# Two node tiles moved from a one-hot product to gathers, the last tile moved to the front, and index lists kept in DRAM

## The chip, the core and the metric

The kernel runs on one core of a Trainium2 chip. The metric is the device time of one execution, in microseconds; every comparison is made with runs of the kernel before on the same chip. The core has a matrix engine (PE, with its weight loads shown apart as PEld), a vector engine (DVE), an activation engine (ACT), a general engine (POOL) that issues the indirect DMAs here, and a sync engine (SP) that issues the plain ones. Each of them works through its own list of instructions strictly in order and waits on semaphores of the others.

## What is computed

The input is a graph of 6250 nodes with 256 features and 200,000 edges sorted by destination. The parts of the reference that matter:

```python
xn = layernorm(x)
x  = x + gcn(edge_index, xn) + linear_attention_block(xn)   # gcn: sum over edges, then W, b, relu
x  = x + mixture_of_experts(layernorm(x))                   # 8 experts, each node goes to one, 977 slots each
# gcn: deg = edges into a node + 1; norm = dinv[src] * dinv[dst]
#      out[n] = relu( sum over edges e into n (and a self loop) of (xn @ W)[src[e]] * norm[e] + b )
```

The sum over the edges is the costly part: for each node, about 32 rows of 256 features from anywhere in the graph have to be added.

## The kernel before

The nodes are cut into 49 tiles of 128 (the last, tile 48, has 106). Tiles are handled in pairs: pair 0 is tiles 0 and 1, pair 23 is tiles 46 and 47, and pair 24 is tile 48 alone. The run has three stages.

**First stage (to about 300 us).** `first_passes` makes the attention sums and queries, pair by pair. `first_chain`, interleaved with it, finds where each node's edges begin (`search`), scales the node features and splits them into bf16 parts (`graph_rows`), and makes the edge lists (`edge_lists`): for gathered tiles `idx` (the source row of each edge) and `rel` (its destination within the tile), for dense tiles `hiT` and `loT` (two numbers that name an edge's source tile and row). All four lists are in SBUF. `checked` counts what would break the fast path into one flag; a branch on that flag ends the stage. With this input the slow path behind the flag is not taken.

**Main stage (about 300 to 1645 us).** Three Python generators are stepped in turn by the loop at the end of the block, and that order is the order in which each engine meets the work (`tc.manual_schedule`):

- `gather()` does the 24 odd tiles. A tile has up to `EB = 34` groups of 128 edges, so there are 24 x 34 = 816 steps. In each step POOL issues one indirect DMA that fetches 128 rows of 2 KB from `g_dram` into `gt` (L891), DVE makes a one-hot matrix `oh` (L895), and `LAG = 7` steps later PE adds `oh` x `gt` to the tile's sum `ps` (L906). `gt` and `oh` have `GB = 9` buffers. `ps` takes one bank of PSUM and has two buffers. A tile begins with two matmuls with an identity for the self loop (L903, L904). `put_sum` takes a finished sum out: an ACT copy (L825) and a DVE add (L827).
- `dense()` does the 25 even tiles. It builds the count matrix A of a tile (49 source tiles x 128 x 128): DVE makes one-hots `lo` and `hi` (L838, L840), 44 of each for a tile, PE multiplies them into `bp` (L874, two buffers, 44 matmuls), and ACT casts `bp` into A (L875, 22 casts). For the tile before it, PE runs the 147 matmuls of A with the features `xs3` (L858). The one-hots are made one step ahead of the matmuls that use them, in 8 buffers of each kind. There are 11 steps to a tile.
- `rounds()` does, for each pair, attention output, feed-forward, graph-layer output, routing logits; every second pair `routing()` finds the expert slot of each node, and POOL scatters the rows to `xbuf` (L984). A round for pair c waits until both tiles of c are summed. Pairs go from 0 to 24.

For each `gather` step the loop runs as many `dense` steps as keep the two in proportion, and `SIDE = 0.74` steps of `rounds`. [...] `mps` 3, `gaps` (for `ps`) 2, `deps` (for `ps_d`) 1, `bups` (for `bp`) 2.

**Last stage (from about 1690 us).** All scatters to `xbuf` have to have landed (`main.close()`); then the eight experts are run, each on its 977 slots, and their rows are scattered to the output. The change does not touch it.

Of the kernel before, what the change touches and what calls it, by code (L numbers as in the profile page):

```python
# [37 lines left out]
ND = (NB + 1) // 2  # L38
NDC = ND // 5
GN = 6  # L40
NG = 22
HID = NB * GN // 2
NGB = NB // 2
# [3 lines left out]
GB = 9  # L47
LAG = 7
SIDE = 0.74
# [13 lines left out]
def graph_block_kernel(  # L63
# [32 lines left out]
    deg_dram = dram.tile([AGR, 1], F32, name="deg_dram")  # L96
    q_dram = dram.tile([len(twos), P, 2, 2 * P], F32, name="q_dram")
# [3 lines left out]
    lists = main.enter_context(tc.tile_pool(name="lists", bufs=1))  # L101
    idx = lists.tile([P, NGC * P], I32, name="idx")
    rel = lists.tile([P, NGC * P], F32, name="rel")
    hiT = lists.tile([P, NDC, 2, 5 * NG], F32, name="hiT")
    loT = lists.tile([P, NDC, 2, 5 * NG], F32, name="loT")
# [136 lines left out]
    V.tensor_scalar(goff, goff, float(EB), float(P), op0=OP.add, op1=OP.mult)  # L242
    nfirst = raw.tile([P, NGC], F32, name="nfirst")
    V.tensor_scalar(nfirst, nth, 2.0 * P, -float(P), op0=OP.mult, op1=OP.add)
# [217 lines left out]
    def edge_lists():  # L462


        fb_ps = sm_ps[:, 64:64 + NGB]
        nc.tensor.matmul(fb_ps, sel0, begin[:, 1:2 * NGB:2], start=True, stop=True)
        fb = raw.tile([P, NGB], F32, name="fb")
        V.tensor_copy(fb, fb_ps)
# [11 lines left out]
        for k, (v, w) in enumerate(((begin, NDC), (pid, NDC), (size, 1))):  # L480
            o = sm_ps[:W, 128 + 16 * k:128 + 16 * k + w]
            for b in range(5):
                rhs = v if w == 1 else v[:, 2 * b:NB:10]
                nc.tensor.matmul(o, sel5[:, b].rearrange("p a g -> p (a g)"), rhs, start=(b == 0), stop=(b == 4))
            t = raw.tile([P, w], F32, name=f"picked{k}")
            V.tensor_copy(t[:W], o)
            picked.append(t)
# [30 lines left out]
        for c in range(NGC):  # L518
            if c % 4 == 0:
                et = [rps.tile([P, 512], F32, name="et_ps", tag="et_ps", bufs=2) for _ in range(2)]  # L520
            gd, gs = got.pop(c)
            gf, gf2 = gd.bitcast(F32), gs.bitcast(F32)
            V.tensor_scalar(gf, gd, nfirst[:, c:c + 1], None, op0=OP.subtract)
            V.tensor_copy(gf2, gs)
            yield
            for e, w in zip(et, (gf, gf2)):
                nc.tensor.transpose(e[:, c % 4 * P:(c % 4 + 1) * P], w, ident)
            ask(c + 2)
            yield
            if c % 4 == 3 or c == NGC - 1:  # L530
                for o, e in zip((rel, idx), et):
                    nc.scalar.copy(o[:, (c - c % 4) * P:(c + 1) * P], e[:, :(c % 4 + 1) * P])
                yield
        for c in range(NDC):
# [18 lines left out]
            for v, o in ((kf, hiT), (lf, loT)):  # L553
# [3 lines left out]
                nc.scalar.copy(o[:, c].rearrange("p h g -> p (h g)"), et_ps[:, :2 * W])  # L557
# [4 lines left out]
    def checked():  # L562
# [12 lines left out]
        wide = raw.tile([1, NGB], F32, name="wide")  # L575
        V.tensor_tensor(wide, begin[:1, 2:2 * NGB + 1:2], begin[:1, 1:2 * NGB:2], op=OP.subtract)
# [131 lines left out]
    with tc.If(flag == 1):  # L708
        with tc.tile_pool(name="gp", bufs=1, side="right") as gp:
# [96 lines left out]
            V.memset(rel, -1.0)  # L806
            V.memset(hiT, 400.0)
# [3 lines left out]
    with tc.tile_pool(name="ga", bufs=GB, side="right") as ga, \  # L811
            tc.tile_pool(name="de", bufs=2, side="right") as de, \
            tc.tile_pool(name="gaps", bufs=2, space=PSUM) as gps, \
            tc.tile_pool(name="deps", bufs=1, space=PSUM) as dps, \
            tc.tile_pool(name="bups", bufs=2, space=PSUM) as bps, \
# [5 lines left out]
        def put_sum(t, ps):  # L821
# [4 lines left out]
            if t % 2:  # L826
                V.tensor_tensor(sums[gi][:, 1, :], ps[:, D:], sums[gi][:, 1, :], op=OP.add)  # L827
            there.add(t)

        def onehots(u, p):  # L830

            c, b = divmod(u, 5)
            o = []
            for g in (2 * p, 2 * p + 1):
                for h in range(2):
                    col = b * NG + g
                    lo = de.tile([P, P], BF16, name="lo", tag="lo", bufs=8)
                    V.tensor_scalar(lo, rowb, loT[:, c, h, col:col + 1], None, op0=OP.is_equal)  # L838
                    hi = de.tile([P, NB * GN], BF16, name="hi", tag="hi", bufs=8)
                    V.tensor_scalar(hi, hib, hiT[:, c, h, col:col + 1], None, op0=OP.is_equal)  # L840
                    o.append((lo, hi))
            return o

        def dense():

            mats, made = {}, None
            acc_ps = None
            half = NG // 2
            for u in range(ND + 1):
                for p in range(half):  # L850
                    if u >= 1 and p >= 1:

                        A = mats[u - 1]
                        if p == 1:
                            acc_ps = dps.tile([P, D], F32, name="ps_d", tag="ps_d")
                        for hi in range((p - 1) * NB // (half - 1), p * NB // (half - 1)):
                            for h in range(3):
                                nc.tensor.matmul(acc_ps, A[:, hi, :], xs3[:, hi, h * D:(h + 1) * D],  # L858
                                                 start=(hi == 0 and h == 0), stop=(hi == NB - 1 and h == 2))
                    coming = None  # L860
                    if u < ND:
                        if p == 0:
                            mats[u] = de.tile([P, NB, P], BF16, name="A", tag="A")
                        coming = (u, p, onehots(u, p))
                    if made is not None:
                        uu, pp, oh = made
                        for i in range(2):
                            g = 2 * pp + i
                            w = GN if g < NG - 2 else 4
                            at = GN * g if g < NG - 1 else P - 4  # L870
                            bp = bps.tile([P, 512], F32, name="bp", tag="bp")
                            for h in range(2):
                                lo, hi = oh[2 * i + h]
                                nc.tensor.matmul(bp[:, :NB * GN], lo, hi, start=(h == 0), stop=(h == 1))  # L874
                            nc.scalar.copy(mats[uu][:, :, at:at + w],  # L875
                                           bp[:, :NB * GN].rearrange("p (s k) -> p s k", k=GN)[:, :, :w])
                        if pp == half - 1:

                            V.tensor_tensor(mats[uu][:, 2 * uu, :], mats[uu][:, 2 * uu, :], identb, op=OP.add)
                    made = coming  # L880
                    if u >= 1 and p == half - 1:
                        put_sum(2 * (u - 1), acc_ps)
                    yield

        def gather():
            tiles = {}
            ps = None
            for j in range(NGT + LAG):
                if j < NGT:
                    gt = ga.tile([P, 2 * D], FR, name="gt", tag="gt")  # L890
                    nc.gpsimd.indirect_dma_start(  # L891
                        out=gt, out_offset=None, in_=g_dram,
                        in_offset=bass.IndirectOffsetOnAxis(ap=idx[:, j:j + 1], axis=0))
                    oh = ga.tile([P, P], FR, name="oh", tag="oh")
                    V.tensor_scalar(oh, rowb, rel[:, j:j + 1], None, op0=OP.is_equal)  # L895
                    tiles[j] = (gt, oh)
                i = j - LAG
                if i >= 0:
                    k, e = divmod(i, EB)
                    t = 2 * k + 1  # L900
                    if e == 0:
                        ps = gps.tile([P, 2 * D], F32, name="ps", tag="ps")
# [11 lines left out]
        def routing(batch, lgt, slots):  # L914

            tiles = [(gi, i) for gi in batch for i in range(twos[gi][1])]
            m = len(tiles)
            t0 = twos[batch[0]][0]
# [5 lines left out]
            def a3(name):  # L924
                return small([P, 4, N_EXP], name)[:, :m, :]

            def a2(name):
                return small([P, 4], name)[:, :m]
# [24 lines left out]
            fore = small([P, 5, N_EXP], "fore")  # L953
# [20 lines left out]
            for gi in batch:  # L974
# [5 lines left out]
            put = small([P, 4], "put", dtype=I32)  # L980
# [10 lines left out]
        def rounds():  # L991


            NGR = len(twos)
            xts, qs, ss, slots = {}, {}, {}, {}
            lgt = None

            def load(gi):
                if gi < NGR:
# [19 lines left out]
            for k in range(-2, NGR):  # L1019
                a = k + 2 if k + 2 < NGR else None  # L1020
                b = k + 1 if 0 <= k + 1 < NGR else None
                c = k if k >= 0 else None
# [3 lines left out]
                if a is not None:  # L1026
                    load(a + 1)
# [48 lines left out]
                if c is not None:  # L1076
                    slot = slots[c] = mx.tile([P, 2, ROW], F32, name="slot", tag="slot", bufs=3)
# [65 lines left out]
                if c is not None:  # L1143
# [5 lines left out]
                    if lgt is None:  # L1149
                        lgt, batch = small([P, 4, N_EXP], "lgt"), []  # L1150
                        if cr < P:
                            V.memset(lgt, 0.0)
                    at = 2 * len(batch)
                    batch.append(c)
# [5 lines left out]
                if c is not None:  # L1160
                    V.tensor_tensor(lgt[:cr, at:at + cn, :], lp[:cr, :cn * N_EXP].rearrange("p (t e) -> p t e", e=N_EXP),
# [12 lines left out]
                if c is not None and (len(batch) == 2 or c == NGR - 1):  # L1174
# [4 lines left out]
        n_dense = (ND + 1) * (NG // 2)  # L1179
# [11 lines left out]
        while any(alive.values()):  # L1191
            step("g", G)
            while alive["d"] and done_d * (NGT + LAG) < n_dense * (j + 1):
# [147 lines left out]
```

## Time and profile before

| | |
|---|---|
| median of 3 runs | 2057.87 us (2054.58 to 2075.5) |
| the profiled execution | 2051.43 us, span of its instructions 2049.6 us |
| main stage, first gather to last gather matmul | 302.1 to 1645.1 us |
| between last gather matmul and first instruction of the last stage | 1645.1 to 1689.3 us |
| busy in 300 to 1645 us: PE, DVE, POOL, ACT | 1097.8, 965.2, 841.0, 407.8 us |
| indirect gathers on POOL | 816, median 0.94 us |

"Busy" is the time in which an engine has an instruction of its own running, taken from one profiled execution. Issue of plain DMAs, waits and branches are not counted. Two instructions of PE that overlap count once, so a busy time is a union; the "mean ns of one" beside it is longer than the union divided by the count, since matmuls are pipelined. A line such as "L874 PE MATMUL bp<-hi,lo" names the line of the code, the engine, the operation, and the tile it writes from the tiles it reads.

### The profile page before, as it was taken

Reading aid. Unit: us, or ns where it says so; the run is one execution under the profiler, and the core shown is the slowest. Engines: PE = TensorE matmul, PEld = TensorE weight load, DVE = VectorE, ACT = ScalarE, POOL = GpSimd, SP = SyncE. Lnnn points to the kernel's source line nnn. Section 1 sums busy time; section 2 is a strip of 40 time slices with the busy share of each in tenths; the row PEclk is TensorE's granted clock in tenths of the full one; section 3 lists DMA queues with packets and bytes.
Section 4 is the critical chain, followed back from the end, with each engine's and each line's share of the span. In section 5 each row is a group of like instructions: output and inputs, shape, how many; then the busy total and the mean of one; then the engine's idle time right before and its main releaser. Section 6 shows DMA issues by size and latency. Waiting matters only on the chain. (4 is left out here: it accounts for less than half of the span.)

```text
span 2049.6 us, 28653 instructions
## 1 busy us (share of the span) xinstructions
PE 1648.4 (80%) x9171; PEld 1203.4 (59%) x9171; DVE 1275.3 (62%) x5337; ACT 700.4 (34%) x1627; POOL 924.3 (45%) x957
## 2 busy tenths in 40 slices
PE   5787866887888888887878787887878737999996
PEld 2454544666666666665656565665656525586774
DVE  5767657677767778686757677776867431232332
ACT  2657952233333333232323232332323112233332
POOL 1022006666666666656656666665665610011111
PEclk9888997999998989898989899898999958999998
DMA  7346767777776677767767676667676615414220
GB/s 214 100 133 196 253 182 194 181 183 196 184 187 173 182 182 189 194 161 193 187 180 180 183 181 169 171 185 183 171 179 170 172 35 188 174 49 146 99 96 19
DMA packets 211319, 337.83 MB, mean 165 GB/s; under 512 B 30047, under 2 KB 79002, under 8 KB 211018
## 3 DMA queue, kind: packets, MB, share of 16 engines
q0 software_dynamic: 125424, 232.93, 44.3%
q1 hardware_dynamic: 85434, 101.74, 15.5%
q8 instruction: 81, 1.33, 0.3%
q10 hardware_dynamic: 288, 1.08, 0.1%
q14 instruction: 92, 0.75, 0.1%
HBM read 278.29 MB, written 60.06 MB: 165 GB/s over the span
## 5 line engine op out<-in xcount | busy, mean ns | idle before, releaser
L891 POOL DMA_INDIRECT gt<-g_dram,idx x816 | 794.8, 974 | 576.1 <-issue 168.7
L858 PE MATMUL ps_d<-xs,A 128*128 128x256 bf16 x3675 | 489.4, 287 | 41.3 <-issue 37.5
L875 ACT CAST A<-bp 128x294 bf16<-128x294 f32 (+1 forms) x550 | 200.6, 401 | 832.8 <-PE bp L874 231.0
L858 PEld LDWEIGHTS <-A 128*128 128x128 bf16 x3675 | 355.5, 103 | 171.5 <-issue 112.9
L906 PE MATMUL ps<-gt,oh 128*128 128x512 f32 x816 | 335.1, 484 | 42.6 <-DMA gt<-g_dram,idx 32.3
L840 DVE TENSOR_SCALAR hi<-hib,hiT 128x294 bf16<-128x294 bf16 x1100 | 351.0, 323 | 1.1 <-issue 1.1
L874 PE MATMUL bp<-hi,lo 128*128 128x294 bf16 x1100 | 216.0, 305 | 120.2 <-ACT A L875 39.6
L838 DVE TENSOR_SCALAR lo<-rowb,loT 128x128 bf16<-128x128 bf16 x1100 | 269.9, 245 | 3.2 <-PE ps_d L858 1.2
L895 DVE TENSOR_SCALAR oh<-rowb,rel 128x128 fp32r<-128x128 bf16 x816 | 207.2, 288 | 76.2 <-remote 30.4
L874 PEld LDWEIGHTS <-lo 128*128 128x128 bf16 x1100 | 109.6, 102 | 180.9 <-issue 57.3
L906 PEld LDWEIGHTS ps<-gt,oh 128*128 128x128 f32 x816 | 153.3, 206 | 76.5 <-DMA gt<-g_dram,idx 37.4
L1285 POOL DMA_INDIRECT out<-rep,who x43 | 42.4, 986 | 314.7 <-DVE rep L1283 226.8
L1257 PE MATMUL hpf<-xet,w1e 128*128 128x512 f32 (+2 forms) x544 | 154.1, 441 | 8.7 <-ACTq L1297 3.5
L1267 PE MATMUL ypf<-w2e,hm 128*128 128x256 f32 (+1 forms) x688 | 151.3, 379 | 0.0
L1267 PEld LDWEIGHTS ypf<-w2e,hm 128*128 128x128 f32 (+1 forms) x688 | 128.9, 188 | 21.9 <-issue 3.1
L1257 PEld LDWEIGHTS hpf<-xet,w1e 128*128 128x128 f32 x544 | 86.5, 193 | 70.0 <-issue 62.9
L1269 DVE TENSOR_TENSOR y<-ypf,fb_s 128x256 f32<-128x256 f32 (+1 forms) x43 | 18.2, 423 | 138.8 <-PE ypf L1267 138.8
L662 PE MATMUL mm<-wqkv_s,xnt 128*128 128x512 f32 (+1 forms) x196 | 101.5, 644 | 0.0
L1259 ACT ACTIVATE hm<-hpf,fb_s 128x512 f32<-128x512 f32 (+2 forms) x136 | 70.9, 525 | 84.6 <-PE hpf L1257 81.2
L1051 DVE TENSOR_SCALAR z<-mm 128x8 f32<-128x8 f32 (+1 forms) x49 | 7.9, 162 | 138.6 <-remote 82.6
L984 POOL DMA_INDIRECT xbuf<-slot,put x49 | 51.8, 1058 | 74.5 <-issue 45.4
L1101 ACT ACTIVATE s<-s,nb,rs 128x256 f32<-128x256 f32 (+1 forms) x98 | 53.6, 599 | 47.3 <-DVE rs_sr L194 29.8
(289 smaller groups left out, 2034.1 us busy)
## 6 DMA issues: line engine op xcount, KB each, us to landing
gt<-g_dram,idx POOLq DMA_INDIRECT x816
g_dram<-two SPq DMA_DIRECT2D x24, 512.0 KB
xt<-in_x SPq DMA_DIRECT2D x42, 256.0 KB
xbuf<-zeros SPq DMA_DIRECT2D x26, 384.0 KB
xe<-xbuf SPq DMA_DIRECT2D x8, 1028.0 KB
w1e<-in_fw SPq DMA_DIRECT2D x8, 1024.0 KB
w2e<-in_fw SPq DMA_DIRECT2D x8, 1024.0 KB
xe<-xbuf SPq DMA_DIRECT2D x8, 771.0 KB
```

Of the source, the lines that this page charges most:

```text
L662: nc.tensor.matmul(kp[:r, :], xnt[:, c, i * r:i * r + r], wqkv_s[:, c, D:3 * D], start=(c == 0), stop=(c == 1))
L838: V.tensor_scalar(lo, rowb, loT[:, c, h, col:col + 1], None, op0=OP.is_equal)
L840: V.tensor_scalar(hi, hib, hiT[:, c, h, col:col + 1], None, op0=OP.is_equal)
L858: nc.tensor.matmul(acc_ps, A[:, hi, :], xs3[:, hi, h * D:(h + 1) * D], start=(hi == 0 and h == 0), stop=(hi == NB - 1 and h == 2))
L874: nc.tensor.matmul(bp[:, :NB * GN], lo, hi, start=(h == 0), stop=(h == 1))
L875: nc.scalar.copy(mats[uu][:, :, at:at + w], bp[:, :NB * GN].rearrange("p (s k) -> p s k", k=GN)[:, :, :w])
L891: nc.gpsimd.indirect_dma_start(out=gt, out_offset=None, in_=g_dram, in_offset=bass.IndirectOffsetOnAxis(ap=idx[:, j:j + 1], axis=0))
L895: V.tensor_scalar(oh, rowb, rel[:, j:j + 1], None, op0=OP.is_equal)
L906: nc.tensor.matmul(ps, oh, gt, start=False, stop=(e == EB - 1))
L1257: nc.tensor.matmul(hp[:, :nn], w1e[:, c, f * P:(f + 1) * P], xet[:, c, at:at + nn], start=(c == 0), stop=(c == 1))
L1259: nc.scalar.activation(hm[:, f, :nn], hp[:, :nn], AF.Relu, bias=fb1_s[:, e * 8 + f:e * 8 + f + 1])
L1267: nc.tensor.matmul(yp[:r, :], hm[:, f, (i - i0) * P:(i - i0) * P + r], w2e[:, f, :], start=(f == 0), stop=(f == DFF // P - 1))
```

## The change

1. Tiles 16 and 32 go from `dense` to `gather`. The tile lists are written out as `GTS` (26 gathered tiles) and `DTS` (23 dense ones), and all index arithmetic that relied on odd and even tiles is replaced (`ahead`, `gone`, `columns_of`, `pid_d`, `begin_d`; the check of widths goes over all tiles).
2. Tile 48 is the first dense tile and its pair the first round. Its logits and its slot row wait in tiles of their own (`lgt_h`, `slot_h`) and join the routing of the last two pairs, so that the last routing has 5 tiles.
3. The lists go from SBUF to DRAM in the first stage (ACT copies into a staging tile `st`, SP writes it out) and come back in pieces during the main stage (`gather_lists`, `dense_lists`: 128 gather steps or 5 dense tiles at a time, two buffers).
4. Buffers and distances: `GB` 9 to 11, `LAG` 7 to 9, one-hots of `dense` made two steps ahead in 12 buffers instead of one step ahead in 8, `bp` three banks instead of two, `ps` one bank instead of two. Between two gathered tiles `gather()` yields once more, so one turn of the loop has no gather. `SIDE` is 0.72.

```diff
+GTS = [t for t in range(NB) if t % 2 or t in (16, 32)]
+DTS = [t for t in range(NB) if t not in GTS]
+ND = len(DTS)
...
+    ahead = raw.tile([P, NGB], F32, name="ahead")
+    V.memset(ahead, 2.0)
+    for k in range(NGB):
+        if GTS[k] - (GTS[k - 1] if k else 0) == 1:
+            V.memset(ahead[:, k:k + 1], 1.0)
...
+    V.tensor_tensor(gone, past, ahead.unsqueeze(1).to_broadcast([P, NGC, NGB]), op=OP.mult)
+    V.tensor_reduce(nfirst, gone, AX.X, OP.add)
+    V.tensor_scalar(nfirst, nfirst, float(P), None, op0=OP.mult)
+    def columns_of(o, v, ids):
+        k = 0
+        while k < len(ids):
+            step = max(1, ids[k + 1] - ids[k]) if k + 1 < len(ids) else 1
+            m = k + 1
+            while m < len(ids) and ids[m] - ids[m - 1] == step:
+                m += 1
+            V.tensor_copy(o[:, k:m], v[:, ids[k]:ids[m - 1] + 1:step])
+            k = m
...
-GB = 9
-LAG = 7
-SIDE = 0.74
+GB = 11
+LAG = 9
+SIDE = 0.72
...
-                for o, e in zip((rel, idx), et):
-                    nc.scalar.copy(o[:, (c - c % 4) * P:(c + 1) * P], e[:, :(c % 4 + 1) * P])
+                for o, e in zip((rel_l, idx_l), et):
+                    st = rw.tile([P, 512], F32, name="st", tag="st")
+                    st = st[:, :(c % 4 + 1) * P] if o is rel_l else st[:, :(c % 4 + 1) * P].bitcast(I32)
+                    nc.scalar.copy(st, e[:, :(c % 4 + 1) * P])
+                    nc.sync.dma_start(o[:, (c - c % 4) * P:(c + 1) * P], st)
...
-                nc.scalar.copy(o[:, c].rearrange("p h g -> p (h g)"), et_ps[:, :2 * W])
+                st = rw.tile([P, 512], F32, name="st", tag="st")
+                nc.scalar.copy(st[:, :2 * W], et_ps[:, :2 * W])
+                nc.sync.dma_start(o[:, c, :], st[:, :2 * W])
...
-            tc.tile_pool(name="gaps", bufs=2, space=PSUM) as gps, \
+            tc.tile_pool(name="gaps", bufs=1, space=PSUM) as gps, \
             tc.tile_pool(name="deps", bufs=1, space=PSUM) as dps, \
-            tc.tile_pool(name="bups", bufs=2, space=PSUM) as bps, \
+            tc.tile_pool(name="bups", bufs=3, space=PSUM) as bps, \
...
+        def part(name, source, dtype=F32):
+            t = chunks.tile([P, source.shape[-1]], dtype, name=name, tag=name)
+            nc.sync.dma_start(t, source)
+            return t
...
+        def dense_lists(c):
+            if c < NDC:
+                his[c] = part("hiT", hi_l[:, c, :]), part("loT", lo_l[:, c, :])
+        def gather_lists(c):
+            if c < NGC:
+                idxs[c] = (part("idx", idx_l[:, c * P:(c + 1) * P], I32), part("rel", rel_l[:, c * P:(c + 1) * P]))
+        gather_lists(0)
+        dense_lists(NDC - 1)
+        dense_lists(0)
+        gather_lists(1)
+        def node_tile(u):
+            return DTS[(u - 1) % ND]
...
+            for n in range((ND + 1) * half + 2):
+                u, p = divmod(n, half)
+                if u < ND:
+                    if p == 0:
+                        mats[u] = de.tile([P, NB, P], BF16, name="A", tag="A")
+                    made.append((u, p, onehots(u, p)))
+                m = n - 2
...
-                    t = 2 * k + 1
+                    t = GTS[k]
                     if e == 0:
+                        if k:
+                            yield
                         ps = gps.tile([P, 2 * D], F32, name="ps", tag="ps")
...
+            order = [NGR - 1] + list(range(NGR - 1))
...
-                a = k + 2 if k + 2 < NGR else None
-                b = k + 1 if 0 <= k + 1 < NGR else None
-                c = k if k >= 0 else None
+                a = order[k + 2] if k + 2 < NGR else None
+                b = order[k + 1] if 0 <= k + 1 < NGR else None
+                c = order[k] if k >= 0 else None
...
+                    if c == NGR - 2:
+                        V.tensor_copy(lgt[:, 4, :], lgt_h)
+                        batch.append(NGR - 1)
...
-                if c is not None and (len(batch) == 2 or c == NGR - 1):
+                if c is not None and cn > 1 and len(batch) >= 2:
                     yield from routing(batch, lgt, slots)
...
-        n_dense = (ND + 1) * (NG // 2)
+        n_dense = (ND + 1) * (NG // 2) + 2
+        n_gather = NGT + LAG + NGB - 1
```

## The prediction

> **What bounds the kernel now.** I read the page's first two parts, then busy time by stage, then who waited for whom on PE and on POOL inside the main stage, then a timeline of POOL, and last the chain that ended last.
>
> Busy time by stage (columns: stretch in us, its length, busy of PE, PEld, DVE, ACT, POOL with counts, granted PE clock, DMA share, GB/s):
>
> ```profile
> 300.00:1645.00 1345.00, 1097.76 (x6926) 827.81 (x6926) 965.23 (x4396) 407.76 (x970) 841.04 (x860) 0.91 0.70 181
> 1645.00:1690.00 45.00, 13.99 (x45) 9.50 (x43) 18.04 (x93) 6.12 (x12) 5.61 (x5) 0.51 0.07 23
> 1690.00:2049.60 359.60, 318.67 (x1360) 230.19 (x1360) 94.87 (x229) 108.02 (x211) 42.40 (x43) 0.95 0.32 110
> ```
>
> The main stage is 1345 of 2050 us, and in it no engine is full: PE is busy 82%. The 45 us after it are nearly empty. The costliest groups of the main stage:
>
> ```profile
> L891 POOL DMA_INDIRECT gt<-g_dram,idx x816 | 794.8, 974 | 576.1 <-issue 168.7
> L858 PE MATMUL ps_d<-xs,A 128*128 128x256 bf16 x3675 | 489.4, 287 | 41.3 <-issue 37.5
> L906 PE MATMUL ps<-gt,oh 128*128 128x512 f32 x816 | 335.1, 484 | 42.6 <-DMA gt<-g_dram,idx 32.3
> L840 DVE TENSOR_SCALAR hi<-hib,hiT 128x294 bf16<-128x294 bf16 x1100 | 351.0, 323 | 1.1 <-issue 1.1
> L874 PE MATMUL bp<-hi,lo 128*128 128x294 bf16 x1100 | 216.0, 305 | 120.2 <-ACT A L875 39.6
> L838 DVE TENSOR_SCALAR lo<-rowb,loT 128x128 bf16<-128x128 bf16 x1100 | 269.9, 245 | 3.2 <-PE ps_d L858 1.2
> L895 DVE TENSOR_SCALAR oh<-rowb,rel 128x128 fp32r<-128x128 bf16 x816 | 207.2, 288 | 76.2 <-remote 30.4
> ```
>
> Who PE and POOL waited for, in 300 to 1645 us:
>
> ```profile
> PE bp L874 <- ACT A L875: 39.6, 26, 3.3
> PE ps_d L858 <- issue: 37.5, 49, 2.2
> PE ps L906 <- DMA gt<-g_dram,idx: 32.3, 24, 2.7
> PE bp L874 <- DVE lo L838: 17.0, 12, 8.5
> PE bp L874 <- DVE hi L840: 14.7, 14, 2.1
> ...
> POOL gt L891 <- PE ps L906: 140.7, 132, 4.4
> ```
>
> PE loses 247 us (1345 - 1098) in short stalls: a bank of `bp` not yet emptied by ACT, one-hots not yet made by DVE, gathered rows not yet landed. POOL mostly waits for PE to free a `gt` buffer. So PE's in-order list with its stalls sets the pace. POOL is the next limit: back to back it issues a gather every 1.24 us,
>
> ```profile
> 1617.07 0.94 POOL L891 DMA_INDIRECT gt<-g_dram,idx  x1 [0.30 <-issue]
> 1618.31 0.94 POOL L891 DMA_INDIRECT gt<-g_dram,idx  x1 [0.31 <-issue]
> ```
>
> and with the mean (0.974 + 0.30 us of issue, and 1.35 for each of the 44 scatters) its 860 operations fill 1099 us, 82% of the stage. The end of the stage, in the chain that ended last:
>
> ```profile
> 1644.63 0.48 PE ps L906
> ...
> 1672.49 0.98 POOL xbuf L984
> ...
> 1682.13 6.68 DMA xbuf<-slot,put
> ```
>
> After the last gather matmul the rounds of pair 23 (scatters up to 1673.5) and of pair 24 (one scatter at 1682.1, landed at 1688.8) run one after the other.
>
> [...] so I count PE's stalls, not its 82%. [...] this trace shows issues of up to 1.59 us against the median 0.94, too few to matter.
>
> **Part 1, two tiles moved.** A dense tile costs PE (489.4 + 216.0)/25 = 28.2 us and DVE (351.0 + 269.9)/25 = 24.8 us. A gathered tile costs PE (335.1 + 16.1 for the identity matmuls)/24 = 14.6 us and DVE (207.2 + 9.7 for the adds)/24 = 9.0 us. Two tiles: PE -27 us, DVE -32 us, ACT -2 x 22 casts. POOL gets 2 x 34 = 68 gathers: +68 x 1.274 = +87 us, to 1185 us. PE is on the path; DVE and ACT are not full; POOL's 87 us are hidden as long as the stage stays longer than 1185 us. DMA: the software queue takes 65% of the engines' time in 1345 us for 860 operations, so 1.02 us each, below POOL's pace.
>
> **Part 2, distances and buffers.** The waits of PE that these can remove: `bp` for ACT 39.6 (a third bank), `bp` for DVE 17.0 + 14.7 + 15.5 in smaller ones (one-hots a step earlier), `ps` for its rows 32.3 (two more steps of lead): 119 us. The other 128 us (issue, the rounds' own chains) stay. I take two thirds, -80 us; the bounds are 0 and -119. A third `bp` bank is paid by the second `ps` bank: PE now waits at each of 25 tile changes until ACT has copied and DVE has added the old sum. In the trace that hand-over ends 0.8 to 6.6 us after the last matmul, mean 2.3; the extra turn leaves PE about two turns of other work, (1098 - 351)/823 = 0.9 us each. What exceeds 1.8 us comes to 0.75 us a tile: +19 us (0 to +40). Behind a waiting PE stand the dense and round matmuls, and ACT and DVE catch up meanwhile.
>
> With this PE needs 1098 - 27 + 247 - 80 + 19 = 1257 us, and POOL would be busy 1185/1257 = 94% of it. Late rows then come oftener than at 82%; I add +10 us, from 32.3 us seen now (0 to +40). Stage: 1267, so -78 us.
>
> **Part 3, the lists through DRAM.** ACT's copies stay, with another target. SP gets 4 + 10 writes in the first stage and 2 x 7 + 2 x 5 reads later. SP's issues take 0.3 to 1.5 us and it waits about 150 us on DVE and ACT between 60 and 300 us, so 14 more cost it nothing by themselves; they stand ahead of `g_dram` stores whose landing DVE waited for (2.7 us once). 2 MB written are about 10 us of DMA at 200 GB/s, beside other work. I take +2 us (0 to +8). The new DVE instructions at the start lie in a 9.2 us wait for the first rows of x. At the branch, the first list pieces have to be read before the first one-hot and gather: one DMA latency, +3 us (SP's first issue is at 299.2, the first gather was at 302.1). Later reads are asked for half a piece ahead, about 80 us: nothing.
>
> **Part 4, last tile first.** One round follows the last gather instead of two. Its last routing has 5 scatters: first at 1668.5 + 0.4 on the old clock, the fifth 4 x 1.31 us later, landing 6.7 us after its issue: 1680.9 instead of 1688.8, -8 us.
>
> **Sum.** The profiled execution took 2051.4 us (span 2049.6). -78 - 8 + 5 = -81 gives 1970. The median of the runs is 6.4 us above that execution: **forecast 1975 us**, which I hold with its own range of 1935 to 2015 at 0.60.
>
> **Rivals.**
> *POOL is the new bound and the stalls vanish:* 1185 plus some 2% for starting and draining, 1210: 2051 - 135 - 3 = 1913, median 1919. For it: POOL waits almost only for PE. Against: 128 us of PE's stalls belong to nothing that is changed. 0.15.
> *The stalls stay:* taking away one cause only shows the next, since DVE waits for PE in the rounds (z L1051, 138 us) as PE does for it. Then 1098 - 27 + 247 + 19 + 10 = 1347, and with -3 the run is at 2050, median 2057: no change. 0.15.
> *The gathers set a slower pace (slower than before):* now an operation takes POOL 1345/860 = 1.56 us with all its waits. If those waits are its own ([...]landing, the 66.9 us marked remote) and not PE's, 928 operations take 1451 us: +106 - 3, median 2161. It decides from 1345/928 = 1.45 us per operation. Against it: runs of 1.24 us as shown, and 140.7 us of its waits ended by PE. 0.10.
>
> **From the cases to the numbers.** The range 1915 to 2050 reaches from the POOL-bound case to the edge of the no-change case and leaves out the slow case and part of that one. Within 1% (2037 to 2078; about what a measurement can tell from no change) lies most of the stalls-stay case and a little of the forecast: 0.14. Slower: 0.11. Faster: 0.75.
>
> **What would show it.** Main stage about 1267 us from first gather to last gather matmul; PE busy near 1070; waits of `bp` for ACT and DVE down from 87 to about 30; a new wait of PE at L903's counterpart for the DVE add, near 19 us; POOL period near 1.36 us; about 36 us instead of 44 between the last gather matmul and the next stage; first gather near 307 us. I am wrong if the hand-over of the single `ps` bank costs several us a tile, or if POOL stops waiting for PE and the rows still come late.

## The result: slower by 3.9%, and where it went

The changed kernel takes 2137.6 us (median of 4 runs, 2131.6 to 2144.28) against 2056.76 us before (2054.58 to 2075.5): ratio 1.0394, 95% interval 1.0361 to 1.0427. The forecast was 1975 us with a range of 1915 to 2050. The profiled execution has a span of 2129.8 us, 80.2 more than before.

One thing has to be known for what follows: the experiments ran on four chips (1, 3, 9 and 12; the record gives no number for the chip of this first pair), and there both kernels take some 9 to 11% less time (before 1876, changed 1907 us) and the change costs 1.7% instead of 3.9%. "The first chip" stands below for where the first pair ran, "the calmer chips" for these four; that the chip itself makes the difference is not shown. So every run is compared by its ratio to the kernel before on its own chip, or with a trace from one of those chips.

Busy time by stage of the changed kernel, with the same columns as in the prediction:

```profile
300.00:1740.00 1440.00, 1106.42 (x6628) 822.92 (x6628) 953.16 (x4310) 393.31 (x930) 909.20 (x928) 0.86 0.71 183
1740.00:1776.00 36.00, 6.88 (x27) 5.15 (x27) 10.07 (x52) 2.78 (x6) 5.62 (x5) 0.60 0.08 26
1776.00:2129.80 353.80, 317.99 (x1360) 231.15 (x1360) 94.62 (x230) 108.19 (x211) 42.36 (x43) 0.96 0.33 112
```

The main stage, first gather to last gather matmul, went from 1343 to 1437.6 us: +95 where -78 was forecast. The stretch after it went from 44 to 36 us, as forecast. PE has 298 matmuls fewer and yet 9 us more of busy time, while its granted clock in the stage fell from 0.91 to 0.86. The groups:

```profile
L965 POOL DMA_INDIRECT gt<-g_dram,idx x884 | 863.5, 977 | 599.9 <-issue 190.4
L934 PE MATMUL ps_d<-xs,A 128*128 128x256 bf16 x3381 | 472.2, 294 | 53.1 <-issue 48.9
L982 PE MATMUL ps<-gt,oh 128*128 128x512 f32 x884 | 360.2, 489 | 41.4 <-DMA gt<-g_dram,idx 25.2
L945 PE MATMUL bp<-hi,lo 128*128 128x294 bf16 x1012 | 194.6, 310 | 77.7 <-ACT A L946 32.1
```

The counts moved as the diff says (816 to 884 gathers, 3675 to 3381 and 1100 to 1012 matmuls), and a gather costs POOL what it did. Who PE waited for in the stage (total us, times, longest):

```profile
PE ps_d L934 <- issue: 48.9, 68, 1.8
PE bp L945 <- ACT A L946: 32.1, 17, 4.6
PE ps L982 <- DMA gt<-g_dram,idx: 25.2, 21, 3.2
...
PE bp L945 <- issue: 19.8, 20, 5.5
...
PE ps L979 <- DVE ag L865: 18.3, 9, 5.9
```

The waits that the change aimed at did shrink (a `bp` bank 39.6 to 32.1, rows 32.3 to 25.2), and the hand-over of the single `ps` bank costs 18.3 us, where I had put 19. But "issue" rows, idle time of PE for which the profile shows no end of a wait, add up to 149 us over all of PE's lines, from 84 before. PE's idle time in the stage rose from 246 to 331 us.

These rows need a caution. A wait is put down to an engine or a DMA by the recorded events of semaphores, and in the main stage the traces of the first pair hold some two fifths of them: 9371 before and 9026 after, where the traces of the same two kernels on chip 3 hold 21,680 and 22,734. So there the page finds no landing of a gather at all, while on chip 3 it does (the changed kernel on the first chip, then on chip 3):

```profile
gt<-g_dram,idx POOLq DMA_INDIRECT x884
gt<-g_dram,idx POOLq DMA_INDIRECT x884, 3.8
```

The instructions themselves are as many in both (28,360), so busy and idle times are not touched. But "issue" and "remote" rows of the first pair can be waits whose end was not recorded, and the table of waits that the prediction worked from is of this kind.

### The profile page after: what moved, and what is told of

It is laid out like the page before. It is cut to its first block, busy times and chain, and to the rows that moved or that the text cites. A ratio compares the mean times of both kernels' runs of the same rounds, so it can differ in the third digit from the quotient of the medians.

```text
span 2129.8 us, 28360 instructions
## 1 busy us (share of the span) xinstructions
PE 1647.1 (77%) x8857; PEld 1194.0 (56%) x8857; DVE 1256.1 (59%) x5232; ACT 682.8 (32%) x1580; POOL 993.2 (47%) x1025
## 5 line engine op out<-in xcount | busy, mean ns | idle before, releaser
L965 POOL DMA_INDIRECT gt<-g_dram,idx x884 | 863.5, 977 | 599.9 <-issue 190.4
L934 PE MATMUL ps_d<-xs,A 128*128 128x256 bf16 x3381 | 472.2, 294 | 53.1 <-issue 48.9
L934 PEld LDWEIGHTS <-A 128*128 128x128 bf16 x3381 | 334.6, 105 | 185.9 <-issue 128.1
L982 PE MATMUL ps<-gt,oh 128*128 128x512 f32 x884 | 360.2, 489 | 41.4 <-DMA gt<-g_dram,idx 25.2
L969 DVE TENSOR_SCALAR oh<-rowb,rel 128x128 fp32r<-128x128 bf16 x884 | 222.8, 288 | 170.4 <-remote 54.6
L907 DVE TENSOR_SCALAR hi<-hib,hiT 128x294 bf16<-128x294 bf16 x1012 | 321.0, 321 | 1.8 <-issue 1.8
L945 PE MATMUL bp<-hi,lo 128*128 128x294 bf16 x1012 | 194.6, 310 | 77.7 <-ACT A L946 32.1
L905 DVE TENSOR_SCALAR lo<-rowb,loT 128x128 bf16<-128x128 bf16 x1012 | 253.6, 251 | 0.4 <-issue 0.4
L982 PEld LDWEIGHTS ps<-gt,oh 128*128 128x128 f32 x884 | 171.7, 212 | 78.9 <-issue 37.8
L1060 POOL DMA_INDIRECT xbuf<-slot,put x48 | 49.7, 1036 | 68.9 <-issue 55.8
L1148 PE MATMUL mm<-gnn_w_s,agt 128*128 128x256 f32 (+1 forms) x196 | 55.2, 431 | 26.6 <-issue 17.4
```

The lines of the kernel that those rows point to most:

```text
L905: V.tensor_scalar(lo, rowb, loT[:, col:col + 1], None, op0=OP.is_equal)
L907: V.tensor_scalar(hi, hib, hiT[:, col:col + 1], None, op0=OP.is_equal)
L965: nc.gpsimd.indirect_dma_start(out=gt, out_offset=None, in_=g_dram, in_offset=bass.IndirectOffsetOnAxis(ap=idxs[c][0][:, w:w + 1], axis=0))
L969: V.tensor_scalar(oh, rowb, idxs[c][1][:, w:w + 1], None, op0=OP.is_equal)
L982: nc.tensor.matmul(ps, oh, gt, start=False, stop=(e == EB - 1))
```

## Experiments

**Theory A:** POOL's own pace per gather is a floor right below the kernel before, so that two more gathered tiles cost time and PE's stalls were worth little. Its pace changed as traces came in, from 1.55 us per operation in the first expectations to 1.30. **Theory B:** PE's list sets the pace, as the prediction had it, and the new order and buffers made it stall more.

### The two kernels side by side on a calmer chip

The changed kernel as it is:

> The changed kernel itself once more, as the partner of the part-wise runs. The first set of part-wise runs gave the kernel before 1877 us where 2057 us had been measured for it, with no stretches in which PE waits for nothing that the profile shows. Theory A (the gathers' pace at 1.31 to 1.35 us per POOL operation binds): ratio to before 1.03 to 1.05 in either surrounding, main stage about 928 operations x 1.35 = 1250 us if the kernel before takes 1877 us. Theory B (PE's stalls alone made it slower): ratio below 1.02 where PE has no unexplained stalls.

1907.35 us, ratio 1.017 (1.0132 to 1.0208): by the number alone this is Theory B's case, and the band of Theory A is missed. Which of the two reasons holds is for the trace and the other runs to say. The kernel before as it is:

> The kernel before once more, for a trace taken in the same surroundings as the part-wise runs. If those surroundings return (1875 us): main stage 1170 to 1180 us, of which 860 POOL operations at the floor of 1.30 us are 1118, so some 55 us of POOL pauses in which it waits for PE (Theory A: the change can gain those at most, and pays 68 x 1.30 = 88 us). Theory B (PE alone the pacer): POOL pauses above 150 us.

1875.35 us. Its main stage, in the columns used above:

```profile
300.00:1470.00 1170.00, 1035.10 (x6923) 800.82 (x6923) 958.56 (x4389) 404.95 (x970) 847.34 (x860) 0.95 0.79 207
```

And that of the changed kernel:

```profile
303.00:1510.00 1207.00, 1032.04 (x6628) 791.60 (x6628) 948.93 (x4310) 388.56 (x930) 911.59 (x928) 0.93 0.83 219
```

These are stages of 1170 and 1207 us, not 1343 and 1438. PE's longest waits there, before and after, are for gathered rows, and in neither kernel does a `bp` bank wait for ACT's casts:

```profile
PE ps L906 <- DMA gt<-g_dram,idx: 95.5, 84, 3.4
PE ps L982 <- DMA gt<-g_dram,idx: 72.8, 75, 4.1
```

POOL's timeline in the changed kernel (start, duration, what, idle before it):

```profile
795.70 0.94 POOL L965 DMA_INDIRECT gt<-g_dram,idx  x1 [0.30 <-PE bp L945]
796.94 0.94 POOL L965 DMA_INDIRECT gt<-g_dram,idx  x1 [0.31 <-DMA gt<-g_dram,idx]
798.18 0.97 POOL L965 DMA_INDIRECT gt<-g_dram,idx  x1 [0.30 <-PE bp L945]
799.46 0.94 POOL L965 DMA_INDIRECT gt<-g_dram,idx  x1 [0.30 <-DMA gt<-g_dram,idx]
```

In this stretch it never stops: only 0.30 us of issue lie between two gathers, whatever is named as releaser. Counting what POOL's pauses of over half a us have beyond that 0.3 us, the changed kernel has 9 us of pauses in the whole stage and 1.29 us per operation without them; the kernel before has 56 us and 1.30. (A pair back to back takes 1.24 us; some issues are longer, in the first pair up to 1.66 us.) The transfers are a weaker candidate for the limit: the DMA engines' share is 0.83 here, and the prediction's pair of gathers starts the same 1.24 us apart where it is 0.70. So the change adds (1206.5 - 9) - (1170.6 - 56) = +83 us of gathering and wins back 47 us of pauses: +36 us of stage. With -7.4 after the stage and +3.5 before it that is the measured +32 us of span. The kernel before lies 5% above POOL's floor, the changed one on it, and the change raises the floor.

### Parts undone

Tiles 16 and 32 dense again:

```diff
-GTS = [t for t in range(NB) if t % 2 or t in (16, 32)]
+GTS = [t for t in range(NB) if t % 2]
```

> The changed kernel with tiles 16 and 32 dense again, all else of the change kept (816 gathers instead of 884, 25 dense tiles instead of 23). Theory A (gathers have a pace of their own, about 1.55 us per POOL operation sustained): 68 fewer gathers take 68 x 1.55 = 105 us off, about 2032 us, main stage near 1330. Theory B (PE's in-order list is the pacer and the new distances and buffers made it stall more): PE gets 27 us more work back, so 2140 to 2165 us.

1852.44 us, ratio 0.9869 (0.983 to 0.9907): 55 us below the changed kernel. Theory B's sign is excluded. The size is half of what A said: 68 gathers at 1.29 us are 88 us, but with the two dense tiles back on PE, POOL pauses for 42 us instead of 9.

The old lead of the gathers and the old share of the rounds; and, to tell the two apart, the old share alone:

```diff
-GB = 11
-LAG = 9
-SIDE = 0.72
+GB = 9
+LAG = 7
+SIDE = 0.74
```

> The changed kernel with the old lead of the gathers (9 buffers, 7 steps instead of 11 and 9) and the old share of the rounds (0.74 instead of 0.72). Theory A (pace of the gathers): no change, 2130 to 2145 us. Theory B (new distances made PE stall more): if the longer lead is the cause, 20 us or more faster, below 2118 us; if it helped as predicted, 10 to 30 us slower.

> The changed kernel with only the share of the rounds back at 0.74. If the share was the cause of the 38 us: ratio to before 1.035 to 1.04. If the shorter lead of the gathers was (rows that PE waits for, 75 us, and buffers that POOL waits for): ratio 1.015 to 1.02, as the changed kernel.

With both, 1945.9 us, ratio 1.0374 (1.0323 to 1.0425): 2% slower than the changed kernel, which Theory A as I had put it did not foresee; Theory B had 10 to 30 us for a lead that helps. With the share alone, 1.0187 (1.013 to 1.0244), as the changed kernel. So the longer lead is worth some 38 us: with 9 buffers POOL pauses for 45 us, with 11 for 9, while PE waits for rows about as long (75 and 73 us). This part of the change works, and through POOL: it shortens waits for a free `gt` buffer (POOL waited 62.0 us for the matmuls of L982 up to 1500 us with 9 buffers, 46.3 us up to 1470 us with 11).

The old banks and no extra turn; and the one-hots one step ahead:

```diff
-            tc.tile_pool(name="gaps", bufs=1, space=PSUM) as gps, \
+            tc.tile_pool(name="gaps", bufs=2, space=PSUM) as gps, \
...
-            tc.tile_pool(name="bups", bufs=3, space=PSUM) as bps, \
+            tc.tile_pool(name="bups", bufs=2, space=PSUM) as bps, \
...
-                        if k:
-                            yield
```

> The changed kernel with two banks for the gathered sums and two for the one-hot products, and without the extra turn at each tile change. Theory A (pace of the gathers): no change, 2130 to 2145 us. Theory B (PE stalls at the single bank's hand-over, seen as 18.3 us of waits for DVE and some unnamed ones): 20 to 60 us faster, 2080 to 2118 us.

```diff
-                m = n - 2
+                m = n - 1
...
-                    lo = de.tile([P, P], BF16, name="lo", tag="lo", bufs=12)
+                    lo = de.tile([P, P], BF16, name="lo", tag="lo", bufs=8)
```

> The changed kernel with the one-hots of the dense tiles made one step ahead in 8 buffers instead of two steps ahead in 12. Theory A (pace of the gathers): no change, 2130 to 2145 us. Theory B, if the two-step order is what makes PE and DVE hold each other up: 20 us or more faster; if it removed waits as predicted, about 20 us slower (the waits of one-hot products for DVE back from 25 to 47 us).

1907.33 us, ratio 1.0164 (1.013 to 1.0199), and 1902.82 us, ratio 1.0122 (1.0087 to 1.0158), against 1.017: neither differs from the changed kernel by more than the intervals. Both undone together:

> The changed kernel with the old banks (two and two, no extra turn) and the one-hots one step ahead in 8 buffers: what stays is the two tiles moved, the lists through DRAM, the longer lead of the gathers and the last tile first. If banks and one-hots add up, 1.04 - 0.023 - 0.027 = ratio 0.99 to before; Theory A (POOL's pace is a floor of about 1.28 us per operation with 928 of them, 1190 us of stage): no more than 10 us below the better of the two alone, ratio 1.005 to 1.015.

1895.22 us, ratio 1.0104 (1.0066 to 1.0142). The third `bp` bank and the second step of lead gained nothing on the calmer chips; if anything they cost half a per cent together, and not in the main stage (1206.5 us with them, 1205.1 without). With the tiles dense too:

> As the run before this one, and tiles 16 and 32 dense too: the kernel before with the last tile first, the longer lead of the gathers and the lists through DRAM. Theory A: 68 gathers fewer x 1.28 to 1.35 = 87 to 92 us less than with the two tiles moved where POOL is the floor, ratio 0.95 to 0.97. Theory B (PE's work and its stalls are the pacer): the same or 27 us slower than with the two tiles moved.

1855.64 us, ratio 0.9888 (0.9847 to 0.9928). What is left is the longer lead, the lists through DRAM and the last tile first, and that is 1.1% faster than before: 13 us in the stage (1171 to 1158) and 9 us after it. Moving the tiles costs this version 40 us. Theory A had said 87 to 92; here too the dense tiles bring pauses of POOL back (41 us).

### Less and more work for PE

In the changed kernel a third of the dense sums, then gather matmuls of half width:

```diff
-                        for h in range(3):
+                        for h in range(1):
...
-                    nc.tensor.matmul(ps, oh, gt, start=False, stop=(e == EB - 1))
+                    nc.tensor.matmul(ps[:, :D], oh, gt[:, :D], start=False, stop=(e == EB - 1))
```

> The changed kernel with two of three matmuls of each dense sum left out (2254 of 3381; only the first part of the three-part sum is added, so the aggregates of the dense tiles are incomplete). PE has about 315 us less work. Theory A (pace of the gathers): main stage stays within 40 us of the changed kernel's, near 928 x 1.27 = 1180 us or above. Theory B (PE is the pacer): 200 us or more shorter, down to POOL's own 1185 us only if it started far above that.

> The changed kernel with the gather matmuls on only the first 256 of 512 columns (the second part of each gathered row is not summed). PE has 884 x 0.24 = 212 us less work. Theory A: stage not shorter than 1190 us, as with a third of the dense sums. And on the granted clock: if the wide fp32 gather matmuls draw the reductions, the clock rises from 0.925 to 0.94 or more; if PE's own idle time (swings between idle and busy) brings them on, it falls towards 0.88, as it did with a third of the dense sums.

1895.51 us, ratio 1.0111 (1.0066 to 1.0156), and 1906.44 us, ratio 1.0187 (1.0117 to 1.0257). With a third of the dense sums:

```profile
308.00:1505.00 1197.00, 886.12 (x4374) 602.04 (x4374) 951.45 (x4310) 390.59 (x930) 910.43 (x928) 0.86 0.84 220
```

2254 matmuls fewer take 146 us off PE's busy time and 10 us off the stage, and PE then waits 189.6 us for gathered rows. In the changed kernel PE's work is not the limit. The same edit on the kernel before, half-width gather sums:

> The kernel before with the gather matmuls on only the first 256 of 512 columns (the second part of each gathered row is not summed): 816 x 0.24 = 196 us less PE work. Theory A (gathers' pace): the main stage falls from 1171 us only to the floor, 860 x 1.30 = 1118 us, so about 1820 us in all, ratio 0.97; that is then the most that taking away PE's stalls could give. Theory B (PE the pacer): 100 us or more shorter, ratio below 0.945. Granted clock: below 0.93 if PE's idle time brings the reductions on.

1858.3 us, ratio 0.9892 (0.9853 to 0.9931), less gain than even Theory A had said:

```profile
301.00:1451.00 1150.00, 984.11 (x6924) 806.62 (x6922) 958.67 (x4392) 404.15 (x970) 851.14 (x860) 0.92 0.81 211
```

I had put this edit at 196 us of PE's work, and that was too much. The gather sums before and after it:

```profile
L906 PE MATMUL ps<-gt,oh 128*128 128x512 f32 x816 | 334.1, 472 | 97.3 <-DMA gt<-g_dram,idx 95.5
L906 PE MATMUL ps<-gt,oh 128*128 128x256 f32 x816 | 250.7, 366 | 114.2 <-DMA gt<-g_dram,idx 110.9
```

They are busy for 83 us less, and PE as a whole for 52 us less (1036 to 984), with the granted clock of the stage at 0.92 instead of 0.95. Of that, 20 us reach the run. The most that the removal of PE's stalls could have given here are POOL's 56 us of pauses; I had forecast 80.

And a fourth matmul in each dense product, in the changed kernel and in the kernel before:

```diff
-                        for h in range(3):
+                        for q in range(4):
+                            h = min(q, 2)
```

> The changed kernel with a fourth matmul in each dense product (the third part is added twice, so the sums of dense tiles are off by it): 1127 matmuls or about 140 us more PE work. Theory A: PE becomes the pacer only past 1206 us; its 1032 + 140 = 1172 busy us and 60 to 130 us of stalls give a stage of 1235 to 1300 us, total 1935 to 2000 us. Theory B (PE was the pacer already): plus the whole 140 us, about 2050 us. On the granted clock: if idle PE brings on the reductions, it rises above 0.93; if PE's work does, it falls below 0.91.

> The kernel before with a fourth matmul in each dense product (the third part is added twice): 1225 matmuls, about 153 us more PE work. PE had 1036 us busy and 135 us idle in a stage of 1171 us. Theory A: the kernel before is nearer to PE's limit than the changed one (which took 27 us more for 141 us), so 60 to 110 us longer, 1935 to 1985 us, ratio 1.03 to 1.06. Theory B: the whole 153 us, ratio 1.08. Granted clock: 0.94 or more if idle PE brings the reductions on.

1932.62 us, ratio 1.0327 (1.0265 to 1.0389): 25 us for 84 us more of PE's busy time (I had put 140). And 1913.44 us, ratio 1.0189 (1.0139 to 1.0239): 35 us, less than I had said, for 103 us more (I had put 153). The stage of the latter:

```profile
298.00:1512.00 1214.00, 1138.88 (x8151) 911.87 (x8150) 963.66 (x4392) 403.75 (x971) 842.05 (x860) 0.97 0.77 200
```

In the kernel before, then, some 40% of what is put on PE or taken off it reaches the stage (43 us of 103, 20 of 52): gathers and PE hold each other up there, and neither theory holds alone. In the changed kernel taking work off PE gives next to nothing (12 us and 1 us).

These runs also bear on the granted clock. In the traces of the first pair its records are at 0.5 or 1.0, nothing between. PE's busy and idle time in the stage and the mean clock of the run:

| kernel | PE busy, idle (us) | clock |
|---|---|---|
| changed, a third of the dense sums | 886, 311 | 0.875 |
| changed, half-width gather sums | 970, 237 | 0.906 |
| changed | 1032, 174 | 0.925 |
| changed, fourth dense part | 1116, 117 | 0.940 |
| before, half-width gather sums | 984, 166 | 0.916 |
| before | 1036, 135 | 0.933 |
| before, fourth dense part | 1138, 75 | 0.948 |

The less PE has to do, the lower its clock in these runs, from 0.948 with 1138 us busy to 0.875 with 886; more work of PE did not go with more time at half speed. In the main stage of the first pair the half-speed records last 3.41 us or a multiple of it: 46 of 47 before and 54 of 59 after are of 3.41, 6.83 or 10.24 us. In the 3.41 us ahead of one PE is busy 32% of the time before and 30% after, against 82 and 77% in the stage as a whole. Why half speed follows idle time is not shown.

### The balance on the other side

If gathers are the floor, tiles should go from gathered to dense. Four versions, all with everything but the longer lead, the lists in DRAM and the last tile first undone; the first two make one odd tile dense, the others two and three (`ahead` is set to the gap wherever it is not 2):

```diff
+GTS = [t for t in range(NB) if t % 2 and t < 46]
...
+GTS = [t for t in range(NB) if t % 2 and t not in (23,)]
...
+GTS = [t for t in range(NB) if t % 2 and t not in (15, 31,)]
...
+GTS = [t for t in range(NB) if t % 2 and t not in (11, 23, 35,)]
```

> As the run with everything back but the last tile first, and tile 47 dense as well: 23 gathered tiles (782 gathers), 26 dense. Theory A (the gathers' pace): 34 x 1.30 = 44 us less, about 1812 us or ratio 0.965, as long as PE (busy 1032 + 13.6, and its 126 us of stalls) is not the pacer. Theory B (PE is the pacer there): 14 us more, about 1870 us, ratio near 1.0. In between if both are near their limit: no gain, ratio 0.985 to 0.99.

> As the run with tile 47 dense too, but with tile 23 in its place, so that the last pair of tiles is not two dense ones (that run's main stage was 37 us shorter and what follows it 17 us longer than with everything back but the last tile first). Theory A (gathers' pace, PE near its limit): main stage near 1121 us again and what follows 394 us, total 1820 to 1830 us, ratio 0.975. Theory B (PE is the pacer): 1850 us or more.

> Two tiles more dense, 15 and 31 (22 gathered tiles, 748 gathers; 27 dense). POOL's floor is 748 + 44 operations x 1.30 = 1030 us. PE needs 1023 + 14 busy and its stalls of 98 us, about 1130 us, so PE is the pacer by now: main stage 1115 to 1140 us, no gain over one tile more dense, ratio 0.97 to 0.985. If the gathers' pace still ruled: 44 us less, ratio 0.955.

> Three tiles more dense, 11, 23 and 35 (21 gathered tiles, 714 gathers; 28 dense). POOL's floor 758 x 1.30 = 985 us. PE 1036 + 14 busy and about 78 us of stalls, so 1128 us of stage, 14 us more than with two: ratio 0.975 to 0.98 if PE rules now; 0.95 if the gathers' pace still does.

| dense tiles more than before | us | ratio to before | main stage | after it | POOL pauses |
|---|---|---|---|---|---|
| none | 1855.64 | 0.9888 | 1158 | 395 | 41 |
| tile 47 | 1841.04 | 0.9839 (0.9794 to 0.9883) | 1121 | 412 | 55 |
| tile 23 | 1844.7 | 0.9836 (0.9782 to 0.989) | 1131 | 405 | 58 |
| tiles 15, 31 | 1824.57 | 0.9711 (0.9672 to 0.975) | 1114 | 410 | 85 |
| tiles 11, 23, 35 | 1828.22 | 0.9729 (0.9675 to 0.9783) | 1098 | 426 | 111 |

Two tiles the other way give a kernel that beats both: 2.9% below before. A third brings no more: the stage ends earlier, but what follows it, where the last rounds finish, grows as much. My 0.975 for tile 23 was wrong: the position of the tile did not bring the time after the stage back.

## Why the prediction was wrong

**The failed step** is the sentence "So PE's in-order list with its stalls sets the pace" and what parts 1 and 2 built on it: that POOL's 87 us stay hidden, and that 80 us of PE's 247 us of stalls turn into time. On the calmer chips the runs show POOL's own pace in its place, with PE close behind it. The 68 gathers more cost 83 us of gathering and the stage can win back only POOL's pauses, 56 us at the most and 47 in fact; a third bank and earlier one-hots give nothing.

On the first chip the sum fails in two terms. It had PE busy for 1098 - 27 us and idle for 247 - 80 + 19 + 10 = 196 us, 1267 in all. Measured were 1106 busy and 331 idle, 1437: 35 us too little in the one and 135 in the other. The stalls that "stay" did not stay, they grew, "issue" rows alone by 65 us. Why is open (see the end of this section).

**Part 1** had the amounts right and the judgement wrong. "POOL's 87 us are hidden as long as the stage stays longer than 1185 us" takes POOL for free until it is full. But PE and POOL wait for each other through the `gt` buffers (in the kernel before on chip 3, PE 95.5 us for rows and POOL 76.4 us for the matmuls of L906), and there 860 operations at 1.30 us are 1118 us of a stage of 1170. The two tiles cost 40 us (with the old banks and one-hots) to 55 us instead of giving 27.

**Part 2.** The new wait for the single `ps` bank was sized right (19; 18.3 in the changed kernel, 12.9 on the calmer chip). The lead of the gathers helped, about 38 us, more than the 32 us of waits for rows that I gave it, through POOL's waits for a free buffer, which I had not counted as a loss. The 119 us of waits that it set out to remove were read from the table with the missing events. In the fuller trace of the same kernel gathered rows have 95.5 us of PE's 135 us of idle time, not 32.3, and ACT's casts none, not 39.6. On chip 3, then, most of what PE waits for are POOL's gathers; how much of the difference is the chip and how much the record is not known. Of the two signs of being wrong that the prediction gave, the second came true on chip 3: POOL hardly waits for PE any more (9 us), and rows still come late (72.8 us).

**Parts 3 and 4** held in the main: the first gather is issued at 302.3 us instead of 302.1 (303.2 instead of 299.7 on chip 3), forecast +5. The last round on the critical path shortened from 44 to 36 us; its last scatters

```profile
1767.59 0.98 POOL L1060 DMA_INDIRECT xbuf<-slot,put  x1 [0.30 <-issue]
1768.88 1.61 POOL L1060 DMA_INDIRECT xbuf<-slot_h,put  x1 [0.31 <-issue]
```

are the end of the five that part 4 laid out (the first two lie 3.2 us apart, not 1.3), and in the chain that ended last only the landing of the fifth follows:

```profile
1768.88 6.69 DMA xbuf<-slot_h,put
```

**The rivals.** "POOL is the new bound" gave a stage of 1210 us, and on the calmer chips it is 1207; it was still a wrong forecast, since the kernel before is at 1170 there, not at 1343. "The gathers set a slower pace" came near the time (2161 against 2137.6), and 928 operations did take 1.55 us each. But POOL's own pace is 1.30, the rest is 240 us of pauses, and "its own waits" was the reason given: the number came near by luck. "The stalls stay" had the nearest account for the first chip, though there they grew; its support was misread, since of the 138 us that DVE sat idle before `z` the trace puts 82.6 to "remote" and 48.8 to PE.

**What the first pair of traces holds beyond that.** On the first chip the changed kernel's stage is 231 us longer than on chip 3: PE is idle for 157 us more and busy for 74 us more. A stretch from there, in PE's timeline:

```profile
756.27 0.38 PE L934 MATMUL ps_d<-xs,A 128*128 128x256 bf16 x2 [1.13 <-issue]
758.40 0.37 PE L934 MATMUL ps_d<-xs,A 128*128 128x256 bf16 x1 [1.75 <-issue]
759.12 0.37 PE L934 MATMUL ps_d<-xs,A 128*128 128x256 bf16 x1 [0.35 <-issue]
759.83 0.43 PE L945 MATMUL bp<-hi,lo 128*128 128x294 bf16 x1 [0.33 <-issue]
```

and the same stretch by windows:

```profile
752.00:754.00 2.00, 2.00 (x15) 1.34 (x13) 1.95 (x10) 0.00 (x0) 1.38 (x3) 1.00 0.82 185
754.00:756.00 2.00, 0.31 (x2) 0.19 (x2) 0.33 (x2) 0.00 (x0) 1.70 (x2) 1.00 0.93 227
...
758.00:760.00 2.00, 0.92 (x3) 0.21 (x2) 0.00 (x0) 0.00 (x0) 0.54 (x1) 0.50 0.86 193
```

PE falls to about one matmul per us (7 from 754 to 760 us), and the clock goes from 1.00 to 0.50: a half-speed record runs from 757.6 to 764.4 us. The dense matmuls of this stretch (L934) carry no wait in the trace, so here the idle time is not a lost record. PE's "issue" idle time is 84 us before and 149 us after on this chip, and none in the traces of either kernel on chip 3; how much of it is of this kind, and how much a wait whose end was not recorded, the traces do not tell apart. Half-speed records take 249 us of the stage before and 382 after (mean clock 0.91 and 0.86), on chip 3 113 and 150 (0.95 and 0.93). So my estimate for the first chip, from this stretch and the 32 and 30% ahead of half-speed records, is that something stops PE, half speed follows, and PE is late for POOL. Here I count 240 us of POOL pauses after and 235 before: 68 gathers more at the floor are 88 us of the 95, and the pauses, which the lead was to shorten, stayed as they were. That is an accounting of two traces and no test: every experiment ran on the calmer chips. What stops PE on that chip, and why that grew with the change, stays open, and so does whether the missing events have to do with it. Nor do the experiments say how the best version would fare there.

## What to carry to other kernels

When two engines hand buffers to each other, an idle share of 18% on one and waits of the other for it do not tell which sets the pace. Price the operations of each with the gap that lies between them (here 860 x 1.30 = 1118 of 1170 us). Pricing alone did not settle it on the first chip, where it gave 82%, so test by taking work off one of them before moving work to the other. And before a table of waits is used, see whether its trace is complete: gathers without a landing time and large "issue" and "remote" rows were the sign here. The move to try is then the one off the engine with the higher floor, until what follows the stage begins to grow.

## Not expected of the hardware

- Less matmul work went with a lower granted clock of PE, 0.925 to 0.875 with 2254 matmuls fewer, and more work with a higher one, 0.940. 1225 matmuls more in the kernel before lengthened its stage by only 43 us.
- The same kernel took 1907 and 2138 us on two chips, with equal time after the main stage (396 and 390 us) and equal gather issues (median 0.94 us). All the difference lies in the main stage (1206 and 1438 us); there POOL's pauses are 9 and 240 us.
